# One root a turn, ordered variance passes and earlier score transposes in the last stage of an axial-attention kernel

## The chip, the core and the metric

The kernel runs on one core of one Trainium2 chip. All arithmetic is float32. A time is that of one execution on the device in microseconds; of several runs the median is given. A profile comes from one further execution, whose span and time are stated beside it.

## The reference

The input is an image batch of 4 x 64 channels x 256 x 256. Layer 0 (layer norms, a gated local branch, channel attention, a convolutional feed-forward part with 8 x 8 Fourier patches) fills the stages before the last. Layer 1 is linear attention along each row, then along each column, then a feed-forward part at each pixel. The last stage computes what follows the row attention, that is, from `hc` on:

```python
def _ln(x, g, b):
    m = x.mean(-1, keepdims=True)
    v = jnp.mean((x - m) ** 2, -1, keepdims=True)
    return (x - m) / jnp.sqrt(v + EPS_LN) * g + b
...
        q = jax.nn.elu(q) + 1.0
        k = jax.nn.elu(k) + 1.0
        q = q / q.mean(axis=3, keepdims=True)
        k = k / k.sum(axis=3, keepdims=True)
        ktv = jnp.einsum('brhcd,brhce->brhde', k, v)
        o = jnp.einsum('brhcd,brhde->brhce', q, ktv)
...
        hc = _ln(h.swapaxes(1, 2), cn_g, cn_b)
        h = h + _lin_attn(hc, col_wq, col_bq, col_wk, col_bk, col_wv, col_bv, col_wo, col_bo).swapaxes(1, 2)
        f = _ln(h, fn_g, fn_b)
        f = jax.nn.gelu(f @ w1.T + b1, approximate=False) @ w2.T + b2
        return jnp.moveaxis(h + f, -1, 1)
```

So every pixel's 64 channels are normalised twice: once for the column attention (the norm enters as a factor 1/sqrt(variance) on the scores), once for the feed-forward part, of the sum `h` with the attention's result.

## The kernel before

The last stage, `stage_d`, goes over 32 groups: 4 images, 8 groups of 32 columns each. A group is one tile `h` of 128 partitions x 32 columns x 2 row halves x 64 channels; four DMAs on SyncE's queue bring it (L1198).

Three generators or functions work on a group, and the loop at the end of the stage staggers them. In turn n, of eight steps r = 0 to 7:

- `scores(n + 1)`: `up` transposes a block of `h` on TensorE (L1236) and copies it to `xT` (ScalarE, L1238); `score` multiplies it by the query and key weights (L1245); `back` turns 4 blocks of scores (L1250). Then the scores are scaled by the reciprocal root, `rs` (L1275), biased (L1276), sent through the Exp of ELU (L695, L696, L1284), and the keys scaled by `rs` once more: `kz` (L1286).
- `result(n)`: keys times values (L1297, on TensorE, from `kz`), sums (L1302), `zm`, `z`, `zn` (L1309 to L1316), a transpose to `zT` (L1319, L1321), `mix` (L702 to L710), `bdm` (L1325), then bias and queries times result (L1331, L1334), added to `h` by VectorE (L1337). After that `h` is normalised into `xf` for the feed-forward part (L1346).
- the feed-forward part of group n - 1, one block of 4 columns a step, in three parts that are one step apart: `turn` transposes `xf` (L1356) and copies (L1358), `first` multiplies by `w1` and takes Gelu on ScalarE (L1367, L1369), `second` transposes `h` into PSUM (L1381), adds the second matmul (L1384), and evicts into the output tile `st` (L1385). After step 7 four DMAs on GpSimd's queue store it (L1391).

`turn` runs two steps ahead of `second` and `first` one, so in step 6 of turn n, `turn` is at the first block of group n itself, which needs its first `xf`.

`spread` is the variance: for a block of 8 columns one sum (`ln_s`, L1207) and one centring (`xc`, L1209) on VectorE, one square on ScalarE (`ln_sq`, L1211), and one sum of the squares on VectorE (`v`, L1215). `rstd` is the root on ScalarE (`ln_d`, L1220) and its reciprocal on VectorE (`ln_r`, L1222). Per turn there are four blocks for the scores and four for the result, and three roots: one of 64 columns for the scores, and one of 32 for each half of the result. ScalarE loads a function table when it goes from Gelu to Sqrt or Exp, and back.

Each generator is advanced twice a step, so there are 16 half steps a turn. `scores` computes its first transposes in half step 0, a score and the next transposes in half steps 2, 3 and 6 to 11, and finishes in 12 and 13. `result` does L1297 in half step 1, the additions to `h` in 4 and 5, and in 6 to 9, alternately, a half's `spread` and its root with the multiplication into `xf`.

TensorE's order is as written (`manual_schedule`). The other engines' queues are ordered by a planner: among instructions that it holds to be ready by its own costs, the one traced first goes first, and a later one that is ready may pass it. The matmul tiles `mm` share 6 PSUM buffers, `sm` 2.

Of the kernel before, what the change touches and what calls it, by code (L numbers as in the profile page):

```python
# [1 line left out]

# [1 line left out]

# [5 lines left out]
F32 = mybir.dt.float32  # L10
AF = mybir.ActivationFunctionType
# [229 lines left out]
def _steps(*gens):  # L241

    live = [g for g in gens if g is not None]
    while live:
        live = [g for g in live if next(g, 0) is None]
# [4 lines left out]
def kernel(ctx: ExitStack, tc: tile.TileContext, x, packs, fd, out, off):  # L250
# [46 lines left out]
    def bc(ap, n):  # L297

        return ap.unsqueeze(2).to_broadcast([ap.shape[0], ap.shape[1], n])
# [6 lines left out]
    def mid_bc(ap, n):  # L306

        return ap.unsqueeze(1).to_broadcast([ap.shape[0], n, ap.shape[1]])
# [856 lines left out]
    def stage_d():  # L1165
        with ExitStack() as cs:
# [27 lines left out]
            def load(b, g):  # L1194
                h = p.tile([128, 32, 2, C], F32, name="h", bufs=4)
                for rh in (0, 1):
                    for j in (0, 1):
                        SY.dma_start(h[:, 16 * j:16 * j + 16, rh, :], hd[b, rh * 128:(rh + 1) * 128, :, 2 * g + j, :])  # L1198
                return h

            def spread(h, ks, v):

                xcs, sqs = [], []
                for k in ks:
                    src = h[:, 8 * k:8 * k + 8].rearrange("p c a e -> p (c a) e")
                    s1 = p.tile([128, 16], F32, tag="ln_s", name="ln_s")
                    V.tensor_reduce(s1, src, AX.X, ALU.add)  # L1207
                    xc = p.tile([128, 16, C], F32, tag="xc", name="xc")
                    V.scalar_tensor_tensor(xc, bc(s1, C), -LN_S, src, ALU.mult, ALU.add)  # L1209
                    sq = p.tile([128, 16, C], F32, tag="ln_sq", name="ln_sq")  # L1210
                    S.activation(sq, xc, AF.Square)  # L1211
                    xcs.append(xc)
                    sqs.append(sq)
                for i, k in enumerate(ks):
                    V.tensor_reduce(v[:, 16 * i:16 * i + 16], sqs[i], AX.X, ALU.add)  # L1215
                return xcs

            def rstd(v, n):
                s3 = p.tile([128, n], F32, tag="ln_d", name="ln_d")
                S.activation(s3, v, AF.Sqrt, bias=eps_t, scale=LN_S)  # L1220
                s4 = p.tile([128, n], F32, tag="ln_r", name="ln_r")
                V.reciprocal(s4, s3)  # L1222
                return s4

# [1 line left out]
            def scores(n):  # L1228
                h = hs[n]
                qp = p1.tile([128, 32, 32], F32, name="qp")  # L1230
                v1 = p1.tile([128, 64], F32, name="v1")

                def up(r):
                    t = mm()
                    for i in range(4):
                        T.transpose(t[:, i * 128:(i + 1) * 128], h[:, r * 4 + i].rearrange("p a e -> p (a e)"), ident)  # L1236
                    xT = p.tile([128, 512], F32, name="xT")
                    S.copy(xT, t)  # L1238
                    return xT

                def score(r, xT, qk):


                    for g in range(4):
                        T.matmul(qk[g * 32:(g + 1) * 32, r % 4 * 128:r % 4 * 128 + 128], cwt, xT.rearrange("p (c n) -> p c n", c=4)[:, :, g * 32:(g + 1) * 32],  # L1245
                                 start=True, stop=True)

                def back(k, qk):

                    V.transpose(qp[:, k * 16:k * 16 + 16].rearrange("p c m -> p (c m)"), qk)  # L1250

                xT = up(0)
                yield
                yield
                qk = sm()
                for r in range(8):
                    if r == 0:
                        spread(h, (0, 1), v1[:, 0:32])
                    if r == 4:
                        back(0, qk)  # L1260
                        qk = sm()
                    score(r, xT, qk)
                    if r < 7:
                        xT = up(r + 1)
                    if r == 3:
                        spread(h, (2, 3), v1[:, 32:64])
                    yield
                    if r == 1:
                        yield
                        yield  # L1270

                back(1, qk)
                rs = rstd(v1, 64)
                u = qp[:, :, 0:16].rearrange("p c (r k) -> p c r k", r=2)
                V.tensor_tensor(u, u, bc4(rs, 2, 8), ALU.mult)  # L1275
                V.tensor_tensor(u, u, cbq.unsqueeze(1).unsqueeze(1).to_broadcast([128, 32, 2, 8]), ALU.add)  # L1276
                e = feature(p1, u, [128, 32, 2, 8])
                yield
                f = p1.tile([128, 2, 2, 32, 4], F32, name="f")
                uv = u.rearrange("p c r k -> p r c k")  # L1280
                ev = e.rearrange("p c r k -> p r c k")
                for rh in (0, 1):
                    for k in (0, 1):
                        V.scalar_tensor_tensor(f[:, rh, k], uv[:, rh, :, k * 4:k * 4 + 4], 1.0, ev[:, rh, :, k * 4:k * 4 + 4], ALU.add, ALU.max)  # L1284
                kz = p1.tile([128, 2, 128], F32, name="kz")
                V.tensor_tensor(kz.rearrange("p r (c h) -> p r c h", h=4), f[:, :, 1], rs.rearrange("p (c r) -> p r c", r=2).unsqueeze(3).to_broadcast([128, 2, 32, 4]), ALU.mult)  # L1286
                fks[n] = f, kz

            def result(n):
# [23 lines left out]
                V.reciprocal(rz, qs[:, 1:2])  # L1313
                zn = p1.tile([128, 65], F32, name="zn")
                G.memset(zn[:, 64:65], 1.0)
                V.tensor_scalar(zn[:, 0:64], z, rz, None, ALU.mult)  # L1316
                yield
                t = mm()
                T.transpose(t[:65, :128], zn, ident)  # L1319
# [2 lines left out]
                yield  # L1322
                m = mix(p1, zT, cgt, qs[:, 0:1])
                bdm = p1.tile([128, 8, 64], F32, name="bdm")
                V.tensor_tensor(bdm, mid_bc(m, 8), bc(mask8, 64), ALU.mult)  # L1325
                yield
                for rh in (0, 1):
                    ts = [mm() for g in range(4)]
                    for g in range(4):
                        r = slice(g * 32, g * 32 + 32)  # L1330
                        T.matmul(ts[g], one[g * 32:g * 32 + 1, :], K("colbo8")[g * 32:g * 32 + 1, :], start=True, stop=False)  # L1331
                    for g in range(4):
                        r = slice(g * 32, g * 32 + 32)
                        T.matmul(ts[g], qT[r, rh * 128:(rh + 1) * 128], bdm[r].rearrange("p c e -> p (c e)"), start=False, stop=True)  # L1334
                    for g in range(4):
                        hh = h[:, 8 * g:8 * g + 8, rh, :]
                        V.tensor_tensor(hh, ts[g].rearrange("p (c e) -> p c e", c=8), hh, ALU.add)  # L1337
                    yield
                for hf in (0, 1):
                    v2 = p.tile([128, 32], F32, name="v2")  # L1340
                    xcs = spread(h, (2 * hf, 2 * hf + 1), v2)
                    yield
                    rs = rstd(v2, 32)
                    for k in (0, 1):
                        xf = p.tile([128, 8, 2, C], F32, name="xf", bufs=6)
                        V.tensor_tensor(xf.rearrange("p c a e -> p (c a) e"), xcs[k], bc(rs[:, k * 16:k * 16 + 16], C), ALU.mult)  # L1346
                        xfs[n, 2 * hf + k] = xf
                    yield

            def turn(i):  # L1350

# [41 lines left out]

            seq = [(b, g) for b in range(B) for g in range(8)]
            N = len(seq)
            hs, fks, xfs, xTs, hgs, sts = {}, {}, {}, {}, {}, {}
            hs[0] = load(*seq[0])
            with tc.manual_schedule(engines={mybir.EngineType.PE}):
                for n in range(-1, N + 1):
                    if 0 <= n + 2 < N:  # L1400
                        hs[n + 2] = load(*seq[n + 2])
                    gs = scores(n + 1) if n + 1 < N else iter(())
                    gr = result(n) if 0 <= n < N else iter(())
                    for r in range(8):
                        i = 8 * (n - 1) + r
                        if 0 <= i + 2 < 8 * N:
                            turn(i + 2)
                        if 0 <= i + 1 < 8 * N:
                            first(i + 1)
                        next(gs, 0)  # L1410
                        next(gr, 0)
                        if 0 <= i < 8 * N:
                            second(i)
                        next(gs, 0)
                        next(gr, 0)
                    _steps(gs, gr)

    stage_d()
# [20 lines left out]
```

## Time and profile before

| | us |
|---|---|
| median of 3 runs | 8637.03 |
| lowest and highest | 8633.92, 8637.6 |
| profiled execution, its time | 8643.85 |
| profiled execution, its span | 8642.1 |
| the last stage, from its first load to the end of the span | 6517 to 8642 |

Over the span TensorE is busy 93%, VectorE 67%, ScalarE 55%, GpSimd 12%; the mean granted TensorE clock is 0.969 of full speed. Columns in the rows that follow: a group gives line, engine, operation, tiles, shapes and count, then busy time in us and mean ns of one, then the idle time of the engine before it and what ended it. A wait gives the engine and line that waited, the one that released it, the total in us, the number of times and the longest. A timeline row gives start and length in us, and the number of instructions merged in it. The window 6650:8500 holds 29 turns of the last stage.

### The profile page before, as it was taken

What the parts mean: (1) busy time and instruction counts of PE and PEld (TensorE: products, weight loads), DVE (VectorE), ACT (ScalarE), POOL (GpSimd) and SP (SyncE); (2) the same over time, 40 slices, a digit from 0 to 9 for tenths busy, and PEclk for the clock granted to TensorE, in tenths of its full rate; (3) what the DMA queues carried; (4) which work ended last, traced back from release to release, by engine and by line L of the source; (5) the groups of instructions that cost most, each with busy time, mean ns of one, the idle gap of its engine ahead of it and who ended that gap; (6) DMA issues with size and microseconds to landing.
All of it is one profiled execution on the core that took longest, in us unless ns stands there. A gap on an engine that the chain in (4) does not pass through costs nothing.

```text
span 8642.1 us, 143479 instructions
## 1 busy us (share of the span) xinstructions
PE 8062.2 (93%) x57518; PEld 4185.5 (48%) x57518; DVE 5829.0 (67%) x8506; ACT 4728.1 (55%) x8291; POOL 1078.3 (12%) x1764
## 2 busy tenths in 40 slices
PE   8999999699999998999999999999997999999998
PEld 6777777444444443333333345555553444444443
DVE  7766666377777775222222258888886888888886
ACT  4455555445555554222222257777774777777776
POOL 1111111212222222000000001101110001010011
PEclk9999999799999999999999999999997999999999
DMA  7777777699999998888888866666643233232332
GB/s 164 160 186 186 182 191 180 177 338 385 393 392 391 389 383 344 298 297 296 296 297 297 298 224 190 187 190 193 187 144 77 59 65 73 59 79 59 62 76 39
DMA packets 1258504, 1832.49 MB, mean 212 GB/s; under 512 B 335600, under 2 KB 1040112, under 8 KB 1196656
## 3 DMA queue, kind: packets, MB, share of 16 engines
q1 hardware_dynamic: 1053296, 1034.63, 40.1%
q0 software_dynamic: 204544, 788.69, 28.8%
q8 instruction: 455, 7.45, 0.3%
q14 instruction: 209, 1.71, 0.1%
HBM read 967.65 MB, written 788.53 MB: 203 GB/s over the span
## 4 chain that ended last, share of the span: by engine, by line
PE 60%; ACT 18%; DVE 16%; issue 4%; DMA 2%; SPq 0%; POOL 0%; ACTq 0%; DVEq 0%; POOLq 0%
PE mm L882 12%; PE mm L889 6%; PE mm L775 4%; PE mm L620 4%; PE mm L824 3%; PE mm L1145 3%; PE mm L1367 2%; ACT xl L812 2%; ACT ln_sq L316 2%; PE mm L1384 2%; ACT hg L1369 2%; DVE xn L314 2%; DVE ln_s L1207 2%; PE mm L1043 2%; DVE xc L1209 2%
## 5 line engine op out<-in xcount | busy, mean ns | idle before, releaser
L915 DVE TENSOR_TENSOR y<-ge,mm 128x512 f32<-128x512 f32 (+1 forms) x640 | 406.0, 635 | 1212.8 <-ACT ge L914 1212.8
L882 PE MATMUL mm<-t,w 128*128 128x512 f32 (+1 forms) x2560 | 1094.2, 566 | 18.8 <-DMA t<-td 18.8
L914 ACT ACTIVATE ge<-mm 128x512 f32<-128x512 f32 (+1 forms) x640 | 354.7, 554 | 1253.7 <-PE mm L889 1253.7
L775 PE MATMUL mm<-gp,wc 128*64 128x510 f32 (+1 forms) x3072 | 701.7, 595 | 90.0 <-DVE xm L785 51.8
L620 PEld LDWEIGHTS mm<-wqk,gp 128*128 128x128 f32 x6144 | 728.5, 197 | 98.8 <-issue 60.8
L882 PEld LDWEIGHTS mm<-t,w 128*128 128x128 f32 x2560 | 455.4, 190 | 647.6 <-issue 437.0
L620 PE MATMUL mm<-wqk,gp 128*128 128x128 f32 x6144 | 762.0, 282 | 1.1 <-POOL gp L589 0.9
L1367 PE MATMUL mm<-xfT,w 64*128 64x512 f32 x2048 | 618.1, 640 | 53.8 <-ACT hg L1369 29.8
L1369 ACT ACTIVATE hg<-mm,b 128x512 f32<-128x512 f32 x1024 | 633.9, 688 | 53.4 <-PE mm L1367 51.6
L830 ACT COPY tb<-mm 128x512 f32<-128x512 f32 x512 | 300.8, 588 | 631.7 <-PE mm L824 631.1
L889 PE MATMUL mm<-t,w 64*64 64x504 f32 (+1 forms) x5120 | 575.6, 555 | 0.0
L824 PE MATMUL mm<-xl,pack_c 64*128 64x512 f32 x2048 | 512.1, 601 | 8.0 <-ACT xl L812 4.7
L1384 PE MATMUL mm<-hg,pack_d 128*64 128x512 f32 x2048 | 514.3, 624 | 0.0
L775 PEld LDWEIGHTS mm<-gp,wc 128*64 128x64 f32 x3072 | 277.5, 137 | 468.8 <-issue 331.2
L316 ACT ACTIVATE ln_sq<-xn 128x1024 f32<-128x1024 f32 x256 | 274.7, 1073 | 365.7 <-DVE xn L314 365.6
L318 DVE TENSOR_REDUCE ln_v<-ln_sq 128x16 f32<-128x1024 f32 x256 | 312.0, 1219 | 185.0 <-ACT ln_sq L316 185.0
L1391 POOL DMA_DIRECT2D out_dram<-st x128 | 209.1, 1638 | 1760.0 <-DVE fe L695 1543.6
L1385 DVE TENSOR_SCALAR st<-mm,pack_d 128x512 f32<-128x512 f32 x256 | 280.5, 1096 | 119.6 <-PE mm L1384 119.3
L828 DVE COPY tb<-mm 128x512 f32<-128x512 f32 x512 | 344.2, 683 | 24.1 <-PE mm L824 18.5
L1367 PEld LDWEIGHTS mm<-xfT,w 64*128 64x128 f32 x2048 | 222.7, 191 | 275.8 <-issue 126.1
L1211 ACT ACTIVATE ln_sq<-xc 128x1024 f32<-128x1024 f32 x256 | 272.7, 1066 | 134.2 <-DVE xc L1209 134.2
L889 PEld LDWEIGHTS mm<-t,w 64*64 64x64 f32 x5120 | 158.1, 132 | 374.4 <-issue 374.4
(458 smaller groups left out, 15244.3 us busy)
## 6 DMA issues: line engine op xcount, KB each, us to landing
t<-td SPq DMA_DIRECT2D x256, 1152.0 KB, 10.2
td<-tb POOLq DMA_DIRECT2D x144, 1024.0 KB, 15.6
td<-tb POOLq DMA_DIRECT2D x288, 512.0 KB, 13.9
yd<-y POOLq DMA_DIRECT2D x128, 1152.0 KB, 10.1
ya<-yd SPq DMA_DIRECT2D x192, 512.0 KB, 8.4
xs<-in_x_dram SPq DMA_DIRECT2D x128, 512.0 KB, 6.9
projd<-pj POOLq DMA_DIRECT2D x256, 256.0 KB, 5.8
gp<-projd SPq DMA_DIRECT2D x128, 512.0 KB, 9.4
```

The costliest lines, as they stand in the source:

```text
L316: S.activation(sq, xc, AF.Square)
L620: T.matmul(qp[:, k * 128:(k + 1) * 128], gp[:, 2 * i + k // 2, at + dx:at + dx + 128], wqk[:, dx, :], start=(dx == 0), stop=(dx == 2))
L775: T.matmul(tv[i * 64:(i + 1) * 64, :, o], wc[2 * pr + i][:, dx, :], gps[i][:, 2 * r:2 * r + 2, i_], start=(dx == 1), stop=False, skip_grou ...
L824: T.matmul(t, inT[q, hf * 128:(hf + 1) * 128], xls[b // 2, s][q, :, 2 * y:2 * y + 2].rearrange("p f y t -> p f (y t)"), start=True, stop=True)
L828: V.tensor_copy(o, i_)
L882: T.matmul(t[:, :n], w[:, 0:128], x_[:, c, :], start=True, stop=False, skip_group_check=True)
L889: T.matmul(t[po:po + 64, :n].rearrange("p (n c) -> p n c", c=64)[:, :, o], w[q:q + 64, 128:192], x_[q:q + 64, c, i_], start=False, stop=Tr ...
L914: S.activation(ge[:, :n], ts[0][k][:, :n], AF.Gelu)
L915: V.tensor_tensor(y[:, c, :].rearrange("p n c -> p (n c)"), ge[:, :n], ts[1][k][:, :n], ALU.mult)
L1367: T.matmul(t, w1[rh * 64:(rh + 1) * 64, k * 128:(k + 1) * 128], xT[rh * 64:(rh + 1) * 64], start=True, stop=True)
L1369: S.activation(g, t, AF.Gelu, bias=b1[:, k:k + 1])
L1384: T.matmul(y[rh * 64:(rh + 1) * 64, :], w2[:, k, :], hg[k * 2 + rh], start=False, stop=(k == 1), skip_group_check=True)
```

## The change

In words:

- `rstd` is replaced by `root(n)`, called once a turn at the start of step 5: one Sqrt and one reciprocal over up to 128 columns, 64 for the scores of group n + 1 and 64 for the result of group n. The reciprocal is given high priority in the planner.
- `spread` no longer returns tiles; the result's centred values are written straight into `xf`, all four blocks in half steps 6 and 7, and multiplied in place by the reciprocal root in half steps 10 and 11.
- The scores' `spread` calls move from `scores` to the loop: blocks 2 and 3 of group n + 1 after step 2, tied by `issue_after` behind `zn` and `bdm` of group n; blocks 0 and 1 of group n + 2 after step 7, tied behind `kz` of group n + 1. `issue_after` orders the block's VectorE instructions after the named one in VectorE's queue and adds no wait for its end.
- `scores` makes its transposes two half steps before their score (in half steps 0 to 3 and 6 to 9), with three `xT` buffers for two.
- The additions to `h` are given high priority.

```diff
+            def spread(h, ks, v, xcs=None):
+
+                sqs = []
+                for i, k in enumerate(ks):
                     src = h[:, 8 * k:8 * k + 8].rearrange("p c a e -> p (c a) e")
                     s1 = p.tile([128, 16], F32, tag="ln_s", name="ln_s")
                     V.tensor_reduce(s1, src, AX.X, ALU.add)
-                    xc = p.tile([128, 16, C], F32, tag="xc", name="xc")
+                    xc = xcs[i].rearrange("p c a e -> p (c a) e") if xcs else p.tile([128, 16, C], F32, tag="xc", name="xc")
...
-            def rstd(v, n):
-                s3 = p.tile([128, n], F32, tag="ln_d", name="ln_d")
-                S.activation(s3, v, AF.Sqrt, bias=eps_t, scale=LN_S)
-                s4 = p.tile([128, n], F32, tag="ln_r", name="ln_r")
-                V.reciprocal(s4, s3)
-                return s4
+            def root(n, lo, hi):
+
+                s3 = p1.tile([128, 128], F32, tag="ln_d", name="ln_d")
+                S.activation(s3[:, lo:hi], vs[n][:, lo:hi], AF.Sqrt, bias=eps_t, scale=LN_S)
+                rss[n] = p.tile([128, 128], F32, tag="ln_r", name="ln_r")
+                with tc.high_priority():
+                    V.reciprocal(rss[n][:, lo:hi], s3[:, lo:hi])
+
+            def variances(n):
+                if n not in vs:
+                    vs[n] = p.tile([128, 128], F32, name="v1")
+                return vs[n]
...
-                    xT = p.tile([128, 512], F32, name="xT")
+                    xT = p.tile([128, 512], F32, name="xT", bufs=3)
...
-                xT = up(0)
-                yield
+                xT = [up(0)]
+                yield
+                xT.append(up(1))
                 yield
                 qk = sm()
                 for r in range(8):
-                    if r == 0:
-                        spread(h, (0, 1), v1[:, 0:32])
                     if r == 4:
                         back(0, qk)
                         qk = sm()
-                    score(r, xT, qk)
-                    if r < 7:
-                        xT = up(r + 1)
-                    if r == 3:
-                        spread(h, (2, 3), v1[:, 32:64])
+                    score(r, xT.pop(0), qk)
+                    if r < 6:
+                        xT.append(up(r + 2))
...
-                rs = rstd(v1, 64)
+                rs = rss[n - 1][:, 0:64]
...
-                V.tensor_tensor(kz.rearrange("p r (c h) -> p r c h", h=4), f[:, :, 1], rs.rearrange("p (c r) -> p r c", r=2).unsqueeze(3).to_broadcast([128, 2, 32, 4]), ALU.mult)
+                marks[n - 1, 0] = V.tensor_tensor(kz.rearrange("p r (c h) -> p r c h", h=4), f[:, :, 1], rs.rearrange("p (c r) -> p r c", r=2).unsqueeze(3).to_broadcast([128, 2, 32, 4]), ALU.mult)
...
-                V.tensor_scalar(zn[:, 0:64], z, rz, None, ALU.mult)
+                marks[n, 1] = V.tensor_scalar(zn[:, 0:64], z, rz, None, ALU.mult)
...
-                V.tensor_tensor(bdm, mid_bc(m, 8), bc(mask8, 64), ALU.mult)
+                marks[n, 2] = V.tensor_tensor(bdm, mid_bc(m, 8), bc(mask8, 64), ALU.mult)
...
-                        V.tensor_tensor(hh, ts[g].rearrange("p (c e) -> p c e", c=8), hh, ALU.add)
+                        with tc.high_priority():
+                            V.tensor_tensor(hh, ts[g].rearrange("p (c e) -> p c e", c=8), hh, ALU.add)
                     yield
                 for hf in (0, 1):
-                    v2 = p.tile([128, 32], F32, name="v2")
-                    xcs = spread(h, (2 * hf, 2 * hf + 1), v2)
-                    yield
-                    rs = rstd(v2, 32)
+                    xf = [p.tile([128, 8, 2, C], F32, name="xf", bufs=6) for k in (0, 1)]
+                    spread(h, (2 * hf, 2 * hf + 1), variances(n)[:, 64 + 32 * hf:96 + 32 * hf], xf)
                     for k in (0, 1):
-                        xf = p.tile([128, 8, 2, C], F32, name="xf", bufs=6)
-                        V.tensor_tensor(xf.rearrange("p c a e -> p (c a) e"), xcs[k], bc(rs[:, k * 16:k * 16 + 16], C), ALU.mult)
-                        xfs[n, 2 * hf + k] = xf
-                    yield
+                        xfs[n, 2 * hf + k] = xf[k]
+                    yield
+                yield
+                yield
+
+                for k in range(4):
+                    xf = xfs[n, k].rearrange("p c a e -> p (c a) e")
+                    V.tensor_tensor(xf, xf, bc(rss[n][:, 64 + k * 16:80 + k * 16], C), ALU.mult)
+                    if k % 2:
+                        yield
...
             hs[0] = load(*seq[0])
+            spread(hs[0], (0, 1), variances(-1)[:, 0:32])
...
+                        if r == 5 and n < N:
+                            root(n, 0 if n + 1 < N else 64, 128 if 0 <= n < N else 64)
                         next(gs, 0)
                         next(gr, 0)
                         if 0 <= i < 8 * N:
                             second(i)
                         next(gs, 0)
                         next(gr, 0)
+
+                        if r == 2 and n + 1 < N:
+                            for k in (2, 3):
+                                with tc.issue_after(marks[n, k - 1].ins) if n >= 0 else nullcontext():
+                                    spread(hs[n + 1], (k,), variances(n)[:, 16 * k:16 * k + 16])
+                        if r == 7 and n + 2 < N:
+                            with tc.issue_after(marks[n, 0].ins):
+                                spread(hs[n + 2], (0, 1), variances(n + 1)[:, 0:32])
```

More of the change, by code (lines that the diff above doesn't have):

```diff
@@ L1 @@
-from contextlib import ExitStack
+from contextlib import ExitStack, nullcontext
 import numpy as np
@@ L1199, in load @@
                 return h
-            def spread(h, ks, v):
-                xcs, sqs = [], []
-                for k in ks:
+            def spread(h, ks, v, xcs=None):
+                sqs = []
+                for i, k in enumerate(ks):
                     src = h[:, 8 * k:8 * k + 8].rearrange("p c a e -> p (c a) e")
@@ L1211, in spread @@
                     S.activation(sq, xc, AF.Square)
-                    xcs.append(xc)
                     sqs.append(sq)
@@ L1215, in spread @@
                     V.tensor_reduce(v[:, 16 * i:16 * i + 16], sqs[i], AX.X, ALU.add)
-                return xcs
-            def rstd(v, n):
-                s3 = p.tile([128, n], F32, tag="ln_d", name="ln_d")
-                S.activation(s3, v, AF.Sqrt, bias=eps_t, scale=LN_S)
-                s4 = p.tile([128, n], F32, tag="ln_r", name="ln_r")
-                V.reciprocal(s4, s3)
-                return s4
+            def root(n, lo, hi):
[8 more added lines that the diff above has]
+                return vs[n]
             def scores(n):
@@ L1230, in scores @@
                 qp = p1.tile([128, 32, 32], F32, name="qp")
-                v1 = p1.tile([128, 64], F32, name="v1")
                 def up(r):
@@ L1336, in result @@
                         hh = h[:, 8 * g:8 * g + 8, rh, :]
-                        V.tensor_tensor(hh, ts[g].rearrange("p (c e) -> p c e", c=8), hh, ALU.add)
+                        with tc.high_priority():
+                            V.tensor_tensor(hh, ts[g].rearrange("p (c e) -> p c e", c=8), hh, ALU.add)
                     yield
                 for hf in (0, 1):
-                    v2 = p.tile([128, 32], F32, name="v2")
-                    xcs = spread(h, (2 * hf, 2 * hf + 1), v2)
+                    xf = [p.tile([128, 8, 2, C], F32, name="xf", bufs=6) for k in (0, 1)]
+                    spread(h, (2 * hf, 2 * hf + 1), variances(n)[:, 64 + 32 * hf:96 + 32 * hf], xf)
+                    for k in (0, 1):
+                        xfs[n, 2 * hf + k] = xf[k]
                     yield
-                    rs = rstd(v2, 32)
-                    for k in (0, 1):
-                        xf = p.tile([128, 8, 2, C], F32, name="xf", bufs=6)
-                        V.tensor_tensor(xf.rearrange("p c a e -> p (c a) e"), xcs[k], bc(rs[:, k * 16:k * 16 + 16], C), ALU.mult)
-                        xfs[n, 2 * hf + k] = xf
-                    yield
+                yield
[5 more added lines that the diff above has]
+                        yield
             def turn(i):
@@ L1395, in stage_d @@
             N = len(seq)
-            hs, fks, xfs, xTs, hgs, sts = {}, {}, {}, {}, {}, {}
+            hs, fks, xfs, xTs, hgs, sts, vs, rss, marks = {}, {}, {}, {}, {}, {}, {}, {}, {}
             hs[0] = load(*seq[0])
+            spread(hs[0], (0, 1), variances(-1)[:, 0:32])
             with tc.manual_schedule(engines={mybir.EngineType.PE}):
```

## The prediction

> **What bounds the kernel now.** I read the page first, then the busy time by stretches, TensorE's waits in the last stage, its timeline over one turn, and the groups of ScalarE and VectorE. The change touches only the last stage, which runs from about 6,520 us to the end.
>
> The page gives the span. The busy time by stretches, for 500 us and for one turn (columns: length, busy time of each engine with its instructions, granted TensorE clock, DMA share, GB/s):
>
> ```profile
> span 8642.1 us, 143479 instructions
> ...
> 7000.00:7500.00 500.00, 462.96 (x2774) 211.14 (x2773) 428.16 (x530) 377.06 (x546) 53.05 (x40) 0.99 0.34 67
> ```
> ```profile
> 7504.80:7568.00 63.20, 59.05 (x351) 27.04 (x349) 54.26 (x68) 47.83 (x70) 6.63 (x5) 0.97 0.34 67
> ```
>
> TensorE is busy 59.05 us of a 63.2 us turn, VectorE 54.26, ScalarE 47.83. Two engines are near full, neither is full: the turn is a loop of hand-overs between them. A turn lasts 63.70 us on average (L1297 first starts at 6687.47 and, 28 turns later, at 8471.18). DMA is at a third and out of it.
>
> TensorE's waits over 6650:8500, 29 turns:
>
> ```profile
> PE sm L1245 <- ACT xT L1238: 58.1, 29, 2.3
> PE mm L1297 <- DVE kz L1286: 28.8, 29, 1.2
> PE mm L1367 <- ACT hg L1369: 27.3, 19, 1.5
> PE mm L1367 <- DVE h L1337: 21.2, 29, 0.7
> PE mm L1381 <- DVE st L1385: 2.2, 12, 0.2
> ```
>
> That is 137.6 us, 4.7 a turn. More is hidden inside groups. From TensorE's timeline of one turn:
>
> ```profile
> 7505.44 2.86 PE L1367 MATMUL mm<-xfT,w 64*128 64x512 f32 x8
> ...
> 7541.15 1.99 PE L1367 MATMUL mm<-xfT,w 64*128 64x512 f32 x8
> ...
> 7548.37 0.53 PE L1245 MATMUL sm<-xT,cwt 128*32 128x128 f32 x8 [1.99 <-ACT xT L1238]
> 7548.83 1.12 PE L1236 MATMUL mm<-pack_k,h 128*128 128x128 f32 x4
> ```
>
> The same eight matmuls take 1.99 us when nothing holds them and 2.86 us behind a late Gelu. From start to start in undisturbed places, L1381 costs 0.53 us, L1384 1.87, L1356 0.53, L1367 1.91: 4.84 a step. A score costs 0.35, its transposes 0.50; the attention's own matmuls 1.85 + 0.91 + 0.26 (L1297, L1302, L1305), 0.11 + 0.43 (L1319, L702), and 2.48 + 1.93 (L1331 with L1334). A turn's sum is 8 x 4.84 + 8 x 0.85 + 7.97 = 53.5 us. So 10.2 us of each 63.7 are lost: half in the waits above, half in stretched groups.
>
> The groups of ScalarE and VectorE in the same window:
>
> ```profile
> L1369 ACT ACT_TABLE_LOAD x116 | 148.8, 1283 | 2.1
> L1220 ACT ACT_TABLE_LOAD x87 | 111.6, 1283 | 1.6
> L696 ACT ACT_TABLE_LOAD x29 | 37.2, 1283 | 0.5
> ...
> L1220 ACT ACTIVATE ln_d<-v,eps_t 128x32 f32<-128x32 f32 x58 | 18.6, 321 | 0.7
> ...
> L1220 ACT ACTIVATE ln_d<-v,eps_t 128x64 f32<-128x64 f32 x29 | 10.1, 348 | 0.3
> ```
> ```profile
> L1346 DVE TENSOR_TENSOR xf<-xc,ln_r 128x1024 f32<-128x1024 f32 x116 | 136.7, 1223 | 1.0
> ...
> L1222 DVE RECIPROCAL ln_r<-ln_d 128x32 f32<-128x32 f32 x58 | 19.0, 327 | 0.0
> ...
> L1222 DVE RECIPROCAL ln_r<-ln_d 128x64 f32<-128x64 f32 x29 | 16.3, 561 | 0.0
> ```
>
> Eight table loads a turn: three roots and one Exp, each followed by a load back to Gelu.
>
> **One root a turn.** Two roots go, and with them four loads: 4 x 1.28 = 5.1 us of ScalarE. The sqrt rows (321 ns at 32 columns, 348 at 64) give about 0.40 at 128, against 0.99 now. ScalarE falls by 5.7 us, to 42. The Trainium skill ("ScalarE: Activation LUTs", What ACT_TABLE_LOAD costs) prices a switch at 1.28 us of load plus 1.38 of drain; in this trace a load begins 0.01 us after the Gelu ahead of it and the next activation 0.02 after it, so no drain is to be had back. By the rule it would be 10.6 us a turn; I take the row. Reciprocals cost 7.3 ns a column between the two rows, so one of 128 columns takes 1.03 us for the present 1.2: VectorE's work stays at 54 us.
>
> The saving reaches TensorE where Gelus stand behind loads. The 1.99 us wait for xT and the 1.4 us waits for hg follow a root pair, and so do most stretched groups. What stays is the Exp pair (1.28 + 0.63 + 1.28 us without a Gelu); I leave 1.0 us for it. The new root falls where TensorE waits anyway, as shown below.
>
> **Scores' transposes two half steps ahead.** The same 8 transposes and copies, one half step earlier. It takes the 2.0 us xT wait away, with the loads or without. The cost is a third xT buffer and one more 0.50 us group in step 0. Taken at zero beyond that; bounded by 0.5 us a turn if PSUM buffers run short, since six are shared.
>
> **Variance passes of the scores.** Twelve VectorE instructions a turn (sum, centring, sum of squares, four times; 1.13 us each from start to start) move. Now all eight sums, the scores' and the result's, start between 7532 and 7564, while VectorE idles in stretches of 2.0, 2.5 and 1.1 us between 7513 and 7532. The change puts six passes behind kz and three each behind zn and bdm. Ahead of the kz wait, two centrings stand today between the ln_r reciprocal and kz (7504.48, 7506.16), so the 1.0 us kz wait should go. A wait isn't added by the ties; what can be late is what queues behind a pass on VectorE: zm, zT, bdm and the h additions, by up to 1.13 us each. bdm has 1.4 us of slack before L1334, zT 2.8. I take 0.4 us a turn, between 0 and 2. The high priority on the additions keeps a pass from standing amid them: today one does (7532.84), and 0.73 us of TensorE's wait follows. No DMA moves; SyncE's loads and GpSimd's stores keep their places.
>
> **What is late next.** A single root needs all four of the result's variances, where today the first half's xf is ready after two (7546.7, for a use at 7556.9). This is the price. From the last h addition: 12 passes x 1.13 = 13.6; one st and one qp transpose between, 1.6; load, sqrt and hand-over 1.8; reciprocal 1.0; first multiply 1.1: 19.1 us. A further st and four Gelus ahead of the load make 22.4. I take 20.0. The additions end 2.6 us behind their matmuls, so xf comes 22.6 us after step 2's end; TensorE's steps 3 to 5 hold 6.54 + 6.54 + 5.54 = 18.6. TensorE then waits about 4.0 us in step 6 for xf, a wait that the trace of before does not have in the steady turns. Behind that L1356 on TensorE stand the step's other matmuls, in order; nothing else is ready to run there. kz now hangs on the same root: reciprocal at 18.9, then L1275, L1276, L695, Exp with its load, L1284 and kz (some 5 us by their rows) among three more multiplications (3.4) and two st (2.0), so at about 29.5 after the additions; L1297 is due at 20.0 + 9.7 + 4.84 + 1.0 = 35.5. Slack 6 us, so no kz wait takes the place of the old one.
>
> As a loop: 20.0, steps 6 and 7 (9.7), step 0 (8.9), step 1 (7.1), step 2 (9.2), the additions 2.6: 57.5 us, or 56.6 to 59.9 by the ends. Add 1.0 for Exp, 0.4 for passes ahead of the chain, and the clock. The Trainium skill speaks against the change here ("TensorE: Matmul & The Clock Gate", Part 1): after an idle window of about 3.4 us the array falls to half rate for about as long. That is 1.7 us lost a turn if each wait trips it. In this trace a 1.99 us wait is followed by slow groups (L1236 1.12 us for 0.66), together some 1.6 us lost, while an equal one at 6656 is followed by none; the 0.97 of this turn holds such a loss already. I take 1.3 of 0 to 1.7. Sum 60.2: 3.5 us less a turn.
>
> Thirty turns: 105 us. At the start, kz of the first group should come some 9 us earlier, the first xf 6 later, and the 14.2 us kz wait at 6618 shrink by about 7; at the end, xf comes late with no scores to cover it, some 6 us. Net 4. The profiled execution took 8643.85 us, span 8642.1, 6.8 above the median of 8637.03; the gain of 109 is taken off the median: 8528.
>
> **Rivals.**
> *Better balanced.* The xf wait is short because scores' passes really vanish from the way and the lower end of the chain (19.1) holds, and the clock stays up: turn 57 to 58.3, gain 5.4 to 6.7 a turn, 8432 to 8471. For it: VectorE and TensorE both need only 54. Against: 54 of 57 leaves VectorE no room.
> *Mostly eaten.* ScalarE's root is queued ahead of ready Gelus and waits for the last variance; behind it stand the Gelus, xT and xfT copies. Today L1220 idles 1.0 us in 87, which speaks against. Priced at 2 us a turn plus the full clock loss (60.2 + 2.0 + 0.4): turn 62.6 to 63.7, 8600 to 8633.
> *Slower.* The ties hold the scores' passes from below only. If they are not placed in the gaps but slip between the last h addition and the root, xf is late by 1.13 us each. The loop is the chain plus 37.5; with the 2.7 us added above it matches 63.7 at a chain of 23.5, three passes above my 20. All six give 26.8 and 67.0 us, 3.3 more a turn: 8736. Against: they come earlier in program order, and VectorE has some 8 us of gaps ahead.
> That the change does not do its work is ruled out for the loads: one root call leaves two.
>
> **How the numbers follow.** As worked, 0.55 (8471 to 8600); better, 0.20; mostly eaten, 0.13, half of it below 8620; slower, 0.12. 0.2%, 17 us, is about what a measurement here can tell from no change: faster 0.82, same 0.06, slower 0.12. The range 8440 to 8640 leaves about 0.04 below and 0.12 above.
>
> **What would show it.** Table loads 8 to 4 a turn; no L1245 wait for xT, kz wait near zero; a new L1356 wait for xf of about 4 us a turn; VectorE's gaps before L1337 filled by L1207 and L1209; L1297 to L1297 near 60.2 us. I am wrong if the xf wait is near zero, if it passes 7 us, or if scores' passes stand between the additions and the root.

## The result, and the profile after

The changed kernel takes 8530.38 us (median of 4 runs, 8526.19 to 8530.97), the kernel before beside it 8637.32 us (8633.92 to 8639.88). The ratio is 0.9875, 95% interval [0.9858, 0.9892]: faster by 1.25%, and 2 us from the forecast of 8528. That closeness is luck: terms of the predicted turn that were 6.3 us too high and others that were 6.4 us too low cancelled, and the wait on which the forecast mainly rested did not come.

The span on the page of the changed kernel, and its busy time over 500 us of the last stage (columns as before):

```profile
span 8524.4 us, 143017 instructions
```
```profile
7000.00:7500.00 500.00, 473.69 (x2893) 217.54 (x2885) 448.77 (x536) 352.99 (x527) 52.99 (x40) 0.99 0.34 68
```

TensorE's busy share rises from 93% to 95%, VectorE's from 86% to 90%, ScalarE's falls from 75% to 71%; the granted clock stays at 0.99. From L1297 to L1297 a turn now takes 60.46 us as a mean of 25 turns (60.34 in most of them); by the same measure it took 63.77 before, and 60.2 was predicted. The span is 117.7 us shorter: L1297 starts at 6665.15 where it started at 6687.47 (22.3 us, the beginning of the stage), the next 29 turns save 100.7 us, and the end gives 5.3 back. The span shrank by more than the medians (107 us) because the profiled execution of before lies 7 us above its median and that of the changed kernel 4 us below.

TensorE's waits over 6650:8400, again 29 turns:

```profile
PE mm L1239 <- DVE st L1390: 49.0, 29, 1.8
PE mm L1239 <- ACT xfT L1363: 20.3, 29, 0.8
PE mm L1386 <- DVE st L1390: 15.3, 58, 0.3
PE mm L1372 <- DVE h L1338: 7.4, 21, 0.4
```

The waits for xT, for kz and for hg are gone. What is left, 92 us for 138, is on other lines: the evictions `st`, which VectorE does late, and the copies `xfT`. There is no wait of L1361 for `xf`, where 4 us a turn were predicted. ScalarE's groups in that window:

```profile
L1374 ACT ACT_TABLE_LOAD x58 | 74.4, 1283 | 1.0
L696 ACT ACT_TABLE_LOAD x29 | 37.2, 1283 | 0.5
L1219 ACT ACT_TABLE_LOAD x29 | 37.2, 1283 | 0.5
```

Four loads a turn for eight, and one root of 402 ns, as estimated. The reciprocal of 128 columns takes 0.95 us (1.03 estimated).

TensorE over one turn, from step 7 to step 6 of the next:

```profile
7503.34 1.94 PE L1389 MATMUL mm<-hg,pack_d 128*64 128x512 f32 x8
...
7505.79 1.99 PE L1372 MATMUL mm<-xfT,w 64*128 64x512 f32 x8
7509.47 0.66 PE L1239 MATMUL mm<-pack_k,h 128*128 128x128 f32 x4 [1.69 <-DVE st L1390]
...
7530.55 1.88 PE L1331 MATMUL mm<-pack_d,one 1*128 1x512 f32 x7
...
7545.33 0.66 PE L1239 MATMUL mm<-pack_k,h 128*128 128x128 f32 x4 [0.79 <-ACT xfT L1363]
...
7555.37 0.66 PE L1361 MATMUL mm<-pack_k,xf 128*128 128x128 f32 x4
```

And VectorE over the same turn:

```profile
7503.45 0.42 DVE L1286 TENSOR_TENSOR kz<-f,ln_r 128x256 f32<-128x256 f32 x1
7503.80 2.34 DVE L1207 TENSOR_REDUCE ln_s<-h 128x16 f32<-128x1024 f32 x2
7506.05 2.35 DVE L1209 SCALAR_TENSOR_TENSOR xc<-ln_s,h 128x1024 f32<-128x1024 f32 x2
7508.32 1.10 DVE L1390 TENSOR_SCALAR st<-mm,pack_d 128x512 f32<-128x512 f32 x1
...
7528.67 1.22 DVE L1214 TENSOR_REDUCE v<-ln_sq 128x16 f32<-128x1024 f32 x1 [1.12 <-ACT ln_sq L1211]
7529.80 2.47 DVE L1338 TENSOR_TENSOR h<-mm,h 128x512 f32<-128x512 f32 x4
...
7533.86 1.22 DVE L1207 TENSOR_REDUCE ln_s<-h 128x16 f32<-128x1024 f32 x1
7535.00 1.88 DVE L1338 TENSOR_TENSOR h<-mm,h 128x512 f32<-128x512 f32 x3
...
7553.93 3.50 DVE L1351 TENSOR_TENSOR xf<-xf,ln_r 128x1024 f32<-128x1024 f32 x3
```

Three things are to be seen. Four passes tied behind kz (which ended at 7503.9) stand ahead of step 7's `st`: TensorE had ended L1389 at 7505.3, `st` starts at 7508.32, and L1239 waits 1.69 us for the PSUM buffer. The last pass tied behind bdm waits 1.12 us for its square, with the four additions to `h` queued behind it; the second L1331 is stretched, to 1.88 us for seven matmuls where the kernel before took 1.14 for eight:

```profile
7530.10 1.14 PE L1331 MATMUL mm<-pack_d,one 1*128 1x512 f32 x8
```

And a sum still stands amid the second four additions. The last addition ends at 7536.88, the first `xf` is ready near 7555.1, and L1361 of step 6 starts at 7555.37: TensorE comes just when `xf` does.

### The profile page after: what moved, and what is told of

Read it like the earlier page. It is cut to its first block, busy times and chain, and to the rows that moved or that the text cites. A ratio compares the mean times of both kernels' runs of the same rounds, so it can differ in the third digit from the quotient of the medians.

```text
span 8524.4 us, 143017 instructions
## 1 busy us (share of the span) xinstructions
PE 8004.1 (94%) x57518; PEld 4175.9 (49%) x57518; DVE 5834.8 (68%) x8443; ACT 4553.9 (53%) x8105; POOL 1075.3 (13%) x1764
## 3 DMA queue, kind: packets, MB, share of 16 engines
q14 instruction: 206, 1.69, 0.1%
## 4 chain that ended last, share of the span: by engine, by line
PE 54%; DVE 26%; ACT 14%; issue 3%; DMA 2%; SPq 1%; POOL 0%; ACTq 0%; DVEq 0%; POOLq 0%
PE mm L882 13%; PE mm L889 6%; PE mm L775 4%; PE mm L620 4%; DVE ln_s L1207 3%; PE mm L824 3%; PE mm L1145 3%; DVE v L1214 2%; DVE st L1390 2%; ACT xl L812 2%; ACT ln_sq L316 2%; DVE xn L314 2%; PE mm L1043 2%; DVE h L1338 2%; DVE xf L1209 2%
## 5 line engine op out<-in xcount | busy, mean ns | idle before, releaser
L1372 PE MATMUL mm<-xfT,w 64*128 64x512 f32 x2048 | 556.3, 636 | 9.8 <-DVE h L1338 8.5
L1389 PE MATMUL mm<-hg,pack_d 128*64 128x512 f32 x2048 | 498.9, 608 | 0.0
L1214 DVE TENSOR_REDUCE v<-ln_sq 128x16 f32<-128x1024 f32 x256 | 307.7, 1213 | 81.9 <-ACT ln_sq L1211 81.7
L824 PEld LDWEIGHTS mm<-xl,pack_c 64*128 64x128 f32 x2048 | 219.0, 186 | 237.0 <-issue 158.1
L812 ACT ACTIVATE xl<-mm,pack_c 128x256 f32<-128x256 f32 x512 | 333.4, 811 | 0.8 <-PE mm L810 0.8
```

What stands on the lines that cost most here:

```text
L812: S.activation(xl.rearrange("p f y (k j t) -> p k t j y f", k=4, t=2)[:, k, a], t.rearrange("p (j y t f) -> p t j y f", j=8, y=8, t=2)[:, ...
L824: T.matmul(t, inT[q, hf * 128:(hf + 1) * 128], xls[b // 2, s][q, :, 2 * y:2 * y + 2].rearrange("p f y t -> p f (y t)"), start=True, stop=True)
L1372: T.matmul(t, w1[rh * 64:(rh + 1) * 64, k * 128:(k + 1) * 128], xT[rh * 64:(rh + 1) * 64], start=True, stop=True)
L1389: T.matmul(y[rh * 64:(rh + 1) * 64, :], w2[:, k, :], hg[k * 2 + rh], start=False, stop=(k == 1), skip_group_check=True)
```

## The experiments

Two theories stood. The order theory: the turn is a loop of hand-overs whose tempo VectorE's queue sets, and the gain comes from where the variance passes stand in it. The table theory: ScalarE's eight table loads a turn set the tempo, and the gain comes from four fewer. All times are medians beside runs of the kernel before on the same chip (8637 to 8639 us); the ratio is to it. The changed kernel itself was timed on another occasion; the differences to it below rest on the kernel before having taken the same time, within 1.5 us, beside each.

**ahead_only**: before, with the early transposes alone.

```diff
-                xT = up(0)
+                xT = [up(0)]
                 yield
+                xT.append(up(1))
                 yield
...
-                    score(r, xT, qk)
-                    if r < 7:
-                        xT = up(r + 1)
+                    score(r, xT.pop(0), qk)
+                    if r < 6:
+                        xT.append(up(r + 2))
```

> The kernel before with only the scores' transposes two half steps ahead (three xT buffers). Order theory (the loop through VectorE's queue sets the turn): the 2.0 us wait of L1245 for xT goes, but VectorE's queue is unchanged and the wait for kz or h takes over most of it; 0.5 us a turn, about 8620 us. Table theory (ScalarE's eight table loads a turn set it): the wait was the mark of a root pair in front of the copy, and hiding it gives all of its 2.0 us a turn, about 8577 us.

Measured: 8592.18 us, 0.9949 [0.9937, 0.9962], 62.47 us a turn. Between the two, nearer to the table theory's figure: 1.3 of the 2.0 us are gained. TensorE's two longest waits in this kernel, over 6650:8350:

```profile
PE mm L1298 <- DVE kz L1287: 34.7, 27, 1.3
PE mm L1368 <- ACT xT L1238: 30.7, 28, 1.4
```

The kz wait grew from 1.0 to 1.3 us, and the copy of xT now holds L1368 (by its PSUM buffer) instead of the score. It is worth more than the order theory gave it, and less than the whole wait.

**one_ahead**: the changed kernel, with that edit undone.

> The changed kernel with only the transposes put back to one half step ahead. Order theory: with the roots' loads out of the way the copy is nearly on time; up to 0.5 us a turn is lost, 8530 to 8545 us. Rival, that the transposes carry the gain: the 2.0 us wait comes back in full, 8590 us.

Measured: 8565.14 us, 0.9918 [0.9905, 0.9932], 35 us above the changed kernel. Both expectations miss; the wait of L1248 for xT returns, twice a turn:

```profile
PE sm L1248 <- ACT xT L1241: 53.1, 57, 1.7
```

The early transposes are worth 46 us alone and 35 on top of the rest, a third to two fifths of the gain of 107.

**three_roots**: the changed kernel, with two idle roots a turn.

```diff
+                        if r in (3, 7) and 0 <= n < N - 1:
+                            extra = p1.tile([128, 1], F32, name="extra")
+                            S.activation(extra, hs[n][:, 0, 0, 0:1] if r == 3 else fks[n + 1][1][:, 0, 0:1], AF.Sqrt, bias=eps_t, scale=0.0)
```

> The changed kernel with two further Sqrt of one column a turn, whose results nobody uses, each with its table load and the load back to Gelu: ScalarE does eight loads a turn again, no data depends on it. Table theory: most of the gain goes, 8620 to 8640 us. Order theory: ScalarE idles some 18 us of a 60 us turn, so the 5.1 us of loads cost 1 us a turn, about 8560 us.

Measured: 8557.36 us, 0.9908 [0.9895, 0.9922], 27 us above the changed kernel. The idle roots' loads were really there, two a turn besides the loads back to Gelu, in ScalarE's groups over 6650:8350, 28 turns:

```profile
L1420 ACT ACT_TABLE_LOAD x56 | 71.8, 1283 | 1.0
```

5.1 us of ScalarE cost 1.0 us of a turn (61.42 for 60.46). The table theory, which wanted 90 us or more, is out as the main cause, as far as the length of the loads goes. No data waits for these idle roots; where real roots fall among the Gelus may cost more (tuned_three, below).

**root_only**: before, with the one root alone. **passes_old**: the changed kernel with the scores' passes back in `scores` (in root_only the transposes are back too).

```diff
                 for r in range(8):
+                    if r == 0:
+                        spread(h, (0, 1), variances(n - 1)[:, 0:32])
...
+                    if r == 3:
+                        spread(h, (2, 3), variances(n - 1)[:, 32:64])
...
-            spread(hs[0], (0, 1), variances(-1)[:, 0:32])
...
-                        if r == 2 and n + 1 < N:
-                            for k in (2, 3):
-                                with tc.issue_after(marks[n, k - 1].ins) if n >= 0 else nullcontext():
-                                    spread(hs[n + 1], (k,), variances(n)[:, 16 * k:16 * k + 16])
-                        if r == 7 and n + 2 < N:
-                            with tc.issue_after(marks[n, 0].ins):
-                                spread(hs[n + 2], (0, 1), variances(n + 1)[:, 0:32])
```

> The kernel before with only the one root a turn: passes of the scores where they were, transposes one half step ahead. Table theory: four loads fewer give most of the gain, 8540 to 8570 us. Order theory: the scores' passes now stand between the last addition to h and the one root, three to six of them at 1.13 us, xf is late and TensorE waits for it: 8640 to 8740 us, not faster than before.

> The changed kernel with the scores' variance passes put back to where they were traced (in scores, after scores 0 and 3); one root and the early transposes stay. Order theory: the passes stand between the additions and the root again, 1.13 us each, and the gain is gone: 8620 to 8720 us. Table theory: the passes' place costs little, 8530 to 8550 us.

Measured: root_only 8770.32 us, 1.0153 [1.014, 1.0167]; passes_old 8781.14 us, 1.0166 [1.0152, 1.018]. Both are slower than the kernel before, and slower than the order theory's ends of 8740 and 8720; turns of 68.0 and 68.6 us. In root_only the wait for xT stays (60.6 us in 25 waits) although four loads a turn are gone. And passes_old, which differs from root_only only by the early transposes, is no faster (11 us slower): there, behind a late `xf`, they gain nothing. TensorE in passes_old at step 6:

```profile
7557.44 1.09 PE L1365 MATMUL mm<-pack_k,xf 128*128 128x128 f32 x4 [8.14 <-DVE xf L1355]
7558.46 3.63 PE L1376 MATMUL mm<-xfT,w 64*128 64x512 f32 x8
```

VectorE ahead of it, between the last addition (ended 7531.14) and the first multiplication into `xf` (7556.09); these are the centrings of the scores' passes that stand there:

```profile
7536.70 1.22 DVE L1209 SCALAR_TENSOR_TENSOR xc<-ln_s,h 128x1024 f32<-128x1024 f32 x1
...
7542.13 1.21 DVE L1209 SCALAR_TENSOR_TENSOR xc<-ln_s,h 128x1024 f32<-128x1024 f32 x1
```

With three sums and two sums of squares there are seven, 7 x 1.13 = 7.9 us, and the first `xf` is 26.1 us behind the addition for 18.2; TensorE waits 8.14 us. The next two groups run at about half rate (1.09 us for 0.66, 3.63 for 1.99), and the granted clock over 7000:8000 is 0.93 for 0.99. This is the slower rival of the prediction, in mechanism, place and about in price: it put six passes at 67.0 us a turn, and here seven took 68.6.

**no_ties**: the changed kernel with `nullcontext()` for each `issue_after`.

> The changed kernel without the order ties: the passes are traced at the new places, but the planner may put them anywhere. In VectorE's queue three of them then stand between the last addition and the reciprocal, and none between zn and the additions. Order theory: xf is 3.4 us later and the gaps ahead of the additions stay open, 2 to 3.4 us a turn, 8590 to 8635 us. Table theory: no difference, 8530 us.

Measured: 8625.66 us, 0.9986 [0.9979, 0.9993], 95 us above the changed kernel; at the upper end of the order theory's span. TensorE:

```profile
7548.60 1.11 PE L1361 MATMUL mm<-pack_k,xf 128*128 128x128 f32 x4 [3.20 <-DVE xf L1351]
```

The last addition ended at 7527.22, so the first `xf` took 21.3 us. Three kernels lie on one line: 18.2 us from the last addition to the first `xf` and no wait (changed), 21.3 and 3.2 us (no_ties), 26.1 and 8.1 us (passes_old). In these three the wait is the chain less 18 us, which is the time that TensorE's own work takes from there to step 6.

**st_tie**: the changed kernel with the centrings of blocks 0 and 1 tied behind step 7's `st`. **tuned**: with two ties more. The core of both:

```diff
-                    V.scalar_tensor_tensor(xc, bc(s1, C), -LN_S, src, ALU.mult, ALU.add)
+                    with tied(centre):
+                        V.scalar_tensor_tensor(xc, bc(s1, C), -LN_S, src, ALU.mult, ALU.add)
...
-                    V.tensor_reduce(v[:, 16 * i:16 * i + 16], sqs[i], AX.X, ALU.add)
+                    with tied(square):
+                        V.tensor_reduce(v[:, 16 * i:16 * i + 16], sqs[i], AX.X, ALU.add)
...
+                    with tied(marks[n, 5]):
+                        spread(h, (2 * hf, 2 * hf + 1), variances(n)[:, 64 + 32 * hf:96 + 32 * hf], xf)
```

`tied` is `issue_after`, or nothing; `centre` is step 7's `st`, `square` bdm for block 2 and the fourth addition for block 3, `marks[n, 5]` the last addition. In st_tie only `centre` is given.

> The changed kernel with one tie more: the centrings of blocks 0 and 1, and what follows them, stand behind step 7's st, which in the changed kernel waits behind four passes. If VectorE's order is what holds TensorE (order theory), the 1.69 us wait of L1239 for st goes and a turn is 1 to 1.7 us shorter: 8480 to 8500 us. If VectorE's amount of work is the bound (54 us of 60), the wait only moves: 8530 us.

> The kernel of st_tie with two ties more: the result's passes start only behind the last addition to h (in the changed kernel one sum stands amid the additions), and the sums of squares of blocks 2 and 3 stand behind bdm and behind the first four additions, so that VectorE does not wait for their squares with the additions queued behind. Order theory: 1 to 1.5 us a turn more than st_tie, near 8440 to 8465 us. Work as the bound: within 0.2% of st_tie.

Measured: st_tie 8470.04 us, 0.9806 [0.9793, 0.982], 58.44 us a turn; tuned 8446.22 us, 0.9778 [0.9765, 0.9792], 57.70 us a turn. Both beat both kernels. TensorE's two longest waits in st_tie, and its one wait in tuned, over 6650:8350:

```profile
PE mm L1244 <- ACT xfT L1368: 21.0, 29, 0.8
PE mm L1391 <- DVE st L1395: 15.7, 59, 0.3
```
```profile
PE mm L1392 <- DVE st L1396: 28.6, 88, 0.5
```

One tie took the 1.69 us wait away and 2.0 us off a turn. The other two took 0.7 us, less than the 1 to 1.5 expected of them: step 2 is 1.2 us shorter, but step 5 is 0.6 longer. VectorE does the same work in all three. So its order, not its amount, held TensorE in the changed kernel. The busy time in tuned, columns as before:

```profile
7000.00:8000.00 1000.00, 981.23 (x6043) 449.86 (x6046) 938.06 (x1132) 730.05 (x1095) 118.36 (x89) 1.00 0.36 75
```

VectorE is busy 938 us of 1000, and there its amount comes near.

**moved_three** and **tuned_three**: the changed kernel and tuned, with the three roots of before.

```diff
-                rs = rss[n - 1][:, 0:64]
+                rs = rstd(vs[n - 1][:, 0:64], 64)
...
-                    spread(h, (2 * hf, 2 * hf + 1), variances(n)[:, 64 + 32 * hf:96 + 32 * hf], xf)
+                    v2 = p.tile([128, 32], F32, name="v2")
+                    spread(h, (2 * hf, 2 * hf + 1), v2, xf)
+                    yield
+                    rs = rstd(v2, 32)
                     for k in (0, 1):
+                        xk = xf[k].rearrange("p c a e -> p (c a) e")
+                        V.tensor_tensor(xk, xk, bc(rs[:, k * 16:k * 16 + 16], C), ALU.mult)
```

> The changed kernel with the three roots of before (one for each half of the result, one for the scores) instead of the one; moved and tied passes and early transposes stay. The first xf then needs two of the result's blocks instead of four. If the chain from the additions to xf sets the turn, hidden in steps 3 to 5, it gets shorter by some 5 us and the kernel is faster than the changed one: 8490 to 8510 us. If the chain is covered, only the four loads more count, as in three_roots: 8555 to 8565 us. If one root is what carried the gain: 8600 us or more.

> The kernel of tuned with the three roots of before, the same question where VectorE's other waits are gone. Chain sets the turn: below 8446 us, some 8420. Chain covered: some 27 us more than tuned for the loads, 8470 us.

Measured: moved_three 8575.87 us, 0.9929 [0.9915, 0.9942], 45 us above the changed kernel; tuned_three 8550.92 us, 0.9902 [0.9888, 0.9915], 105 us above tuned. In both the first `xf` is ready 13 us after the last addition, for 18 to 19, and nothing is gained: the chain is covered there. But three roots cost more than the 27 us of three_roots, most of all in tuned, and both times lie above what was expected for a covered chain (8555 to 8565, 8470). In tuned_three TensorE waits again for Gelus:

```profile
PE mm L1374 <- ACT hg L1376: 27.1, 40, 0.9
```

Two root pairs fall within one step, at 7513.4 and 7517.1, with a single Gelu between. That this placing makes up the rest of the cost is likely from the timeline; no run moved the pairs alone.

## Why the prediction was right, step by step

The direction and the size came as forecast, and most of the signs did: four loads a turn for eight, no wait for xT, no steady wait for kz, and passes in VectorE's gaps ahead of the additions. The main step did not. The prediction said that it was wrong if the wait for `xf` is near zero, and that wait is zero. So the turn is not closed by the loop from the additions through `xf` that the prediction summed, and its 60.2 us for a measured 60.46 is a right sum of partly wrong terms.

**The floor and the loss.** The sum of 53.5 us for a turn of TensorE stands: the changed kernel's undisturbed groups have the same lengths. The loss fell from 10.2 to 7.0 us a turn.

**One root.** Loads, root and reciprocal measured as worked out. Once the passes stand elsewhere one root is worth 45 us (moved_three against the changed kernel); alone it costs 132 us (root_only). It is good only together with the moved passes, which the prediction said through its slower rival.

**Early transposes.** Predicted to remove 2.0 us a turn; worth 1.3 alone and 0.9 on top of the rest.

**The passes ahead of the chain.** This term was mis-sized: 0.4 us a turn taken, between 0 and 2. In the changed kernel step 0 takes 10.87 us for a floor of 8.86, and step 2 10.48 for 9.25; passes ahead of `st` and of the additions stand at both places, 3.2 us together, and st_tie and tuned won 2.8 back. The prediction named zm, zT, bdm and the additions as what queues behind a pass; `st` was missing, and so was the wait of a pass for its own square.

**The wait for xf.** Predicted at 4.0 us, measured at none, since both sides of that difference were off. The chain took 18.2 us, not 20.0. And TensorE's steps 3 to 5 took 21.7 us (7533.65 to 7555.37), not the 18.6 of a TensorE that nothing holds. The two are separate: steps 3 to 5 take about as long where `xf` is ready early (from the start of step 3's `turn` to that of step 6's, medians of 22 turns, in us).

| kernel | last addition to first `xf` | steps 3 to 5 without a wait for `xf` | wait for `xf` |
|---|---|---|---|
| tuned_three | 13.0 | 21.4 | 0 |
| moved_three | 13.0 | 22.7 | 0 |
| changed | 18.2 | 21.7 | 0 |
| tuned | 18.8 | 22.1 | 0 |
| no_ties | 21.3 | 22.0 | 3.2 |
| passes_old | 26.1 | 22.0 | 8.1 |

So the 3.1 us above 18.6 are not the price of a late `xf` in another place. In the timelines the `st`, the `xfT` copies and the Gelus of those steps stand behind the result's passes and squares, and TensorE is held 0.2 to 0.8 us at a time; that this is the cause is likely, but no run moved them. They are what made the wait vanish: the chain begins 3.2 us after step 3 does and takes 18.2, so against 18.6 us of TensorE's work it would have left a wait of 2.8. The prediction took that work at its undisturbed length, and this is the step of it that failed. The changed kernel sits near the corner: the longer chains of no_ties and passes_old are paid for in the wait.

**The clock and Exp.** 1.3 and 1.0 us were added; neither came. The 1.3 was read from a turn in which the 1.99 us wait for xT was followed by slow groups. Of the 28 such waits of before in 6650:8400 only 10 were followed so; in the changed kernel 2 of the 29 waits of 1.69 us were, and its granted clock is 0.99. Slow groups followed 24 of 28 waits of 3.2 us (no_ties) and all 26 of 8.1 us (passes_old). The Trainium skill ("TensorE: Matmul & The Clock Gate", Part 1) puts the fall to half rate behind an idle window of about 3.4 us; the 8.1 us waits agree, but slow groups came here behind shorter waits too, so its figure is no safe bound for a single wait. Behind the Exp pair L1372 takes its unstretched 1.99 us. The two terms and the 4.0 us wait were too high by 6.3 us, the passes, steps 3 to 5 and steps 6 and 7 (10.2 for 9.7) too low by 6.4: the total of 60.2 owes its closeness to that.

**The high priorities.** The prediction held that they keep a pass from amid the additions. They don't: the sum at 7533.86 stands there. The tie in tuned moved it.

**The ends.** Predicted as 4 us to the good in all, measured as 17 (22.3 less 5.3); the loss at the end is about the predicted one (6), the start gained more. Between the medians only 107 of the span's 117.7 us are seen, for the reason given with the result, so this surplus does not show in the forecast's error.

## What to carry to other kernels

Where two engines are each nine tenths busy, look in the busier helper's queue for what stands ahead of each instruction that the bound engine waits for: three order ties there were worth another 84 us without a single operation less. A merged operation (one root for three) frees one engine and lengthens a chain on another; here it paid only once whatever else stood in that chain was moved out, and the time that the waiting engine's other work fills, here 18 us, tells how long the chain may be. That time is to be read from a trace, stretched groups and all, and not from a sum of undisturbed lengths. And a moved step must be checked against every eviction in its new neighbourhood, not only against the chain that it feeds.

## What the runs showed that I had not expected

The same edit changed sign with its company: one root is worth 45 us less time with the passes moved and 132 us more without. A pass that sums what another engine has yet to square holds all behind it: VectorE idled 2.1 us a turn for two of them (0.98 and 1.12 us). And the same wait of about 2 us on TensorE was followed by slow matmuls in one turn and by none in the next: a loss read from one turn is not the loss of a mean turn.
